# Linear attention with a sparse feed-forward layer: scores of two head groups in one go, and the fourth group of a step behind the output products that follow

## The chip, the cores and the metric

The kernel runs on one core of a Trainium2 chip. The metric is the device time of one execution in microseconds (us); "time" below means that. Five engines work side by side: PE (TensorE, the matmuls; PEld is its weight load), DVE (VectorE), ACT (ScalarE), POOL (GpSimd) and SP (SyncE, which here only issues DMAs). Each executes its own instructions in the order in which they were written; an instruction that must wait for another engine or for a DMA holds up everything behind it on its engine.

## The reference, cut to what matters

```python
x = x + _layernorm(_L0_attn_ref(_layernorm(x), Wq, Wk, Wv, Wo))      # x: 2 x 1024 x 512, float32
x = x + _layernorm(_L0_ffn_ref(_layernorm(x), w_gate, w_up, w_down))
...
# attention: 16 query heads, 4 key/value heads of 128; q and k get rotary positions, then elu + 1
state = state + k_s[..., :, None] * v_s[..., None, :]
z = z + k_s
num = jnp.einsum('bhe,bhed->bhd', q_s, state)
den = jnp.einsum('bhe,bhe->bh', q_s, z)[..., None] + EPS
out = num / den                                                       # then out @ Wo.T
# feed-forward: silu(x w_gate) * (x w_up), 2 of every 4 kept, then w_down
```

The attention is causal and linear: each position sees a running sum of k times v. A kernel may take it by chunks: within a chunk a masked matrix of scores q k, and from earlier chunks the state.

## The kernel before, in words

**Tiling.** The 1024 positions are cut into NC = 8 chunks of 128. The heads are taken in two passes of 8 query heads and 2 key/value heads, so there are STEPS = 16 steps: steps 0 to 7 are the first pass, 8 to 15 the second. A step n has four groups i = 0 to 3 (line 811: a batch b and a key/value head j), each with 4 query heads. After the attention follow four rounds of the feed-forward layer, which the change does not touch.

**Products.** Every large product (q, k and v, the output product "O" with Wo, the feed-forward products) is made by seven products of half-size factors (`chain`, line 507), in the order 1, 2, 6, 5, 7, 4, 3; their sums are made on ACT and DVE. `kv_products(n)` and `q_products(n)` make step n's k, v and q one step ahead, in step n-1. `o_products(n)` makes step n's output product; five of its seven products are issued in step n+1 and the last two (numbers 4 and 3) at the start of step n+2, by `run(previous, 2)` (line 1955).

**One group.** `features` (line 767) turns a raw q into its features on DVE, POOL and ACT. `moved` (line 629) then transposes it: DVE transposes 32x32 blocks into the tile `blocks`, SP writes them to a DRAM buffer `qb`, and four more DMAs of SP read it back as the tile `qT`. `scores(n, i)` (line 924) waits for `qT` of its group, makes the scores on PE into the PSUM tile `sc` (one buffer) and has DVE multiply them by the mask into `am` (one buffer). From the second chunk of a pass on, the scores of a group are two matmuls of a tile with 128 rows and 64 columns, 256 columns streamed in each. `attend(n, i)` (line 1022) multiplies q with the state (lines 1057) and the masked scores with v (line 1068, tiles of 64 rows), and makes the next group's change of the state (line 996); DVE and ACT then divide (`divided`, line 1089 and 1093), and `moved` sends the result through DRAM (`ob`) into the tile `of`, the left factor of the output products.

**The order on PE** is written out by hand in the loop over n (line 1920). In a step n of the first pass after the first it reads: last two output products of step n-2; products of q and k/v for step n+1 with `outputs(0)` and `outputs(1)` in between; two output products of step n-1; `outputs(2)`; two more; the transpose of k (`k_transposed(n+1)`); one more; `outputs(3)`. Steps 0 to 5 also hold two transposes of x (`step_input`). The function `outputs(i)` (line 1928) is:

```python
attend(n, i)
if i < 3:
    scores(n, i + 1)
elif 0 < n < STEPS - 1:
    scores(n + 1, 0)
```

So each `scores` stands alone behind an `attend`, one group ahead of its use. Behind the loop the last step is written out once more (lines 2030 to 2060), with `ffn_transposed` for the first transposes of the feed-forward layer.

**The order on the other engines** comes from a planner (`Plan`, line 36): processes ask for an engine with an estimated length and a rank, PE's issue times drive its clock, and the result is a fixed order per engine. Nothing in it is decided at run time. SP's one queue holds all DMAs: the reads and writes above, the weights of the second pass (`load_pass`, line 1269), x, the rotary table, and the preparation of the feed-forward weights, `prepare_all` (line 400), which loads 1 MB at a time, lets POOL make sums and stores 1 MB.

Of the kernel before, what the change touches and what calls it, by code (L numbers as in the profile page):

```python
# [13 lines left out]
ALU = mybir.AluOpType  # L14
PSUM = bass.MemoryType.PSUM

P = 128
B, S, DM = 2, 1024, 512
H, KVH, HD = 16, 4, 128
REP = H // KVH  # L20
DFF = 2048
NIC = DM // P
NC = S // P
# [88 lines left out]
def kernel(  # L112
# [16 lines left out]
    nc = tc.nc  # L129
# [9 lines left out]
    causal = const.tile([P, P], F32, name="causal")  # L139
# [11 lines left out]
    mask = const.tile([P, 64], F32, name="mask")  # L151
# [131 lines left out]
    STEPS = 2 * NC  # L283
# [175 lines left out]
    plan = Plan()  # L459
# [36 lines left out]
    def transposed(src, kind, *names):  # L496

        t, name, before = bank(kind, [P, 4, P])

        def issue():  # L500
            for j in range(4):
                nc.tensor.transpose(t[:, j, :], src[:, j, :], ident)

        plan.pe(0.45, issue, *before, *names)
        return t, name
# [304 lines left out]
    kf, kT, v1, qT = {}, {}, {}, {}  # L810
    GROUPS = ((0, 0), (1, 1), (0, 1), (1, 0))
# [109 lines left out]
    states, mids = {}, {}  # L921
    am, o = {}, {}

    def scores(n, i):
        b, j = GROUPS[i]
        plan.need(("qT", n, i), ("kT", n), *(("am", *k) for k in list(scored)))
        first = n % NC == 0
        sc = ps_sc.tile([P, 4, REP, 32], F32, tag="sc", name="sc")
        us = 4 if first else 2

        def issue():
            if first:
                nc.tensor.matmul(
                    sc.rearrange("p u h t -> p (u h t)"),
                    kT[n][:, 2 * b + j, :],
                    qT[n, i].rearrange("p u e -> p (u e)"),
                    start=True,
                    stop=True,
                )
                return  # L940
            for r in range(2):
                half_ = slice(64 * r, 64 * r + 64)
                nc.tensor.matmul(
                    sc[half_, 0:2].rearrange("p u h t -> p (u h t)"),
                    kT[n][:, 2 * b + j, half_],
                    qT[n, i][:, 2 * r : 2 * r + 2, :].rearrange("p u e -> p (u e)"),
                    start=True,
                    stop=True,
                    tile_position=(0, 64 * r),
                )  # L950

        def masked():
            yield "dve", 0.8 if first else 0.45, 0
            t = qp.tile([P, 4, REP, 32], F32, tag="am", name="am", bufs=1)
            of_ = (causal if first else mask).rearrange("p (u t) -> p u t", t=32).unsqueeze(2)
            nc.vector.tensor_tensor(
                t[:, 0:us], sc[:, 0:us], of_.broadcast_to([P, us, REP, 32]), ALU.mult
            )
            am[n, i] = t
            plan.signal(("am", n, i))  # L960

        plan.pe(0.87 if first else 0.6, issue, ("qT", n, i), ("kT", n), *(("am", *k) for k in scored))
        scored[:] = [(n, i)]
        plan.spawn(masked())

    scored, attended = [], []
# [156 lines left out]
    def o_factor(n, i):  # L1123

        k = (0, 2, 1, 3)[i]
        return factor(n, k, 2 if k in (0, 2) else 1)

    def o_free(n, i):

        k = n - 2 if i < 2 else n - 1  # L1130
        names = [("o", k, (1, 3, 2, 5)[i])] if k >= 0 else []
        return names + ([("of", k, 6)] if i == 2 and k >= 0 else [])

    def o_transposed(n, i, kind="a"):

        plan.need(("divided", n, i), *o_free(n, i))
        pt, name = transposed(o.pop((n, i)), kind, ("divided", n, i))

        def copy():
            yield "act", 0.65, 0  # L1140
            to = o_factor(n, i).rearrange("p h (u t) -> p h u t", t=32)
            nc.scalar.copy(to, pt.rearrange("p u (h t) -> p h u t", t=32))
            plan.signal(name)
            plan.signal(("of", n, i))

        plan.spawn(copy())
# [149 lines left out]
    def run(g, times):  # L1296
        for _ in range(times):
            next(g, None)
# [554 lines left out]
    with tc.manual_schedule(engines={E.PE, E.Pool, E.SP, E.DVE, E.Activation}):  # L1853
# [63 lines left out]
        run(qpr, 2)  # L1917
        opr = None
        part = 0
        for n in range(STEPS):  # L1920
            more = n + 1 < STEPS

            def next_part():
                nonlocal part
                plan.signal(("part", part))
                part += 1

            def outputs(i, n=n):
                if n not in (NC - 2, NC):
                    next_part()  # L1930
                attend(n, i)
                if i < 3:
                    scores(n, i + 1)
                elif 0 < n < STEPS - 1:
                    scores(n + 1, 0)

            if 0 < n < NC - 2:
                next_part()
            if n + 3 < NC:
                plan.spawn(load(n + 3, "x"))  # L1940
            if n + 2 < STEPS:
                if n + 2 < NC:
                    plan.spawn(step_normalize(n + 2, ("root", n)))
                else:
                    plan.spawn(step_input_again(n + 2))
            if n + 2 == NC:
                plan.spawn(load_pass(1, "wq", 2, 512, q_quarter, wq_dram, ("q", n + 1)))
                plan.spawn(load_pass(0, "wkv", 2, 256, kv_quarter, wkv_dram, ("k", n + 1)))
            elif n == NC:
                plan.spawn(load_pass(2, "wo", 4, 256, o_quarter, wo_dram, ("o", n - 1)))  # L1950
            previous, opr = opr, (o_products(n - 1) if n > 0 else None)
            if n > 0:
                plan.spawn(o_sums(n - 1))
            if n > 1:
                run(previous, 2)
            if not more:
                break
            kvp, qpr = kv_products(n + 1), q_products(n + 1)
            run(qpr, 1)
            if n == 0:  # L1960
                run(qpr, 1)
                run(kvp, 1)
                k_transposed(0, "e")
                q_transposed(0, 0, "e")
                run(qpr, 1)
            else:
                run(kvp, 1)
                run(qpr, 1)
                if n == 1:
                    k_transposed(1, "e")  # L1970
                    first_state(1, 0)
                elif n == NC + 1:
                    first_state(n, 0)
                run(qpr, 1)
                if n == 1:
                    scores(1, 0)
                    q_transposed(1, 1)
                    o_transposed(0, 3, "e")
            run(kvp, 1)
            plan.signal(("root", n))  # L1980
            if n > 0:
                outputs(0)
            else:
                scores(0, 0)
            if n + 2 < STEPS:
                plan.spawn(load(n + 2, "rope"))
            run(kvp, 1)
            run(qpr, 1)
            if n == 0:
                q_transposed(0, 1)  # L1990
                outputs(0)
            run(kvp, 1)
            run(qpr, 1)
            run(kvp, 1)
            if n == 0:
                q_transposed(0, 2)
                outputs(1)
                run(kvp, 1)
                run(qpr, 1)
                q_transposed(0, 3)  # L2000
                run(kvp, 1)
                step_input(2, 0, "a")
                outputs(2)
                step_input(2, 1, "a")
                run(qpr, 1)
                outputs(3)
            else:
                outputs(1)
                run(qpr, 1)
                run(kvp, 1)  # L2010
                run(qpr, 1)
                run(kvp, 1)
                run(opr, 2)
                outputs(2)
                if n + 2 < NC:
                    step_input(n + 2, 0, "a")
                run(opr, 2)
            if n + 2 == STEPS:
                plan.need(("prepared",), *(("features", n + 1, i) for i in range(4)))
                rctx.close()  # L2020
                begin_ffn()
            if n > 0:
                k_transposed(n + 1)
                run(opr, 1)
                if n + 2 < NC:
                    step_input(n + 2, 1, "a")
                outputs(3)


        o_transposed(n - 1, 3)  # L2030
        outputs(0)
        run(opr, 2)
        outputs(1)
        o_transposed(n, 0)
        for tt, kind in enumerate("eba"):
            ffn_transposed(tt, kind)
        run(opr, 3)
        o_transposed(n, 1)
        outputs(2)
        run(opr, 1)  # L2040
# [5 lines left out]
        opr = o_products(n)  # L2046
# [97 lines left out]
```

## Time and profile before

| what | value |
|---|---|
| median of three runs | 1283.44 us (1282.59 to 1283.59) |
| the profiled execution: time / span of its instructions | 1281.84 us / 1280.1 us |
| PE busy | 1251.9 us, 98% of the span |
| DVE, ACT, POOL busy | 67%, 36%, 27% |
| mean granted clock of PE | 0.996 |
| DMA queue of SP: packets' share of the 16 DMA engines | 62.4% |

The time around the span is 1.74 us. The profiled execution was 1.60 us faster than the median of the three runs. In the page's lines, "out<-in" names the tiles that an instruction writes and reads, Lnnn is a line of the kernel, and a figure in square brackets is idle time of the engine before the instruction with what ended it. Matmuls of 32-bit floats appear as two records each, so "x4" in the scores are two matmuls.

### The profile page before, as it was taken

The numbers are of one execution on the slowest core, as the hardware profiler recorded it, in microseconds if no ns is written. First come the engines' busy times: TensorE is split into PE (matmuls) and PEld (weight loads), VectorE is DVE, ScalarE is ACT, GpSimd is POOL, SyncE is SP. The second block draws the span as 40 slices with busy tenths as digits, with TensorE's granted clock in tenths as the row PEclk, the third lists the DMA queues.
The fourth block names the chain that finished last, engine by engine and source line by source line (L and its number), as shares of the span: only waits on it lengthen the run. The fifth ranks groups of instructions, "written<-read, shape, count | busy, mean of one in ns | idle before, by whom it ended". The sixth has DMA issues, their size and how long they took to land. (4 is left out here: it accounts for less than half of the span.)

```text
span 1280.1 us, 17815 instructions
## 1 busy us (share of the span) xinstructions
PE 1251.9 (98%) x6092; PEld 991.7 (77%) x6092; DVE 855.1 (67%) x1577; ACT 457.2 (36%) x909; POOL 341.5 (27%) x263
## 2 busy tenths in 40 slices
PE   7899999999999999999999999999999999999998
PEld 4566776777677766777678888888888888888886
DVE  7886877876566886778754588326971687426763
ACT  3653444443334444435443333113220343023211
POOL 4543443532232454455421101001100110010010
PEclk9998999999999999999999999999999999999999
DMA  7265678569767877676584499367546756465312
GB/s 266 94 232 191 224 233 274 194 214 280 243 219 206 290 235 232 233 241 207 174 244 149 138 253 257 115 190 220 152 136 209 245 152 193 154 190 173 109 41 91
DMA packets 280297, 252.60 MB, mean 197 GB/s; under 512 B 19216, under 2 KB 239376, under 8 KB 277520
## 3 DMA queue, kind: packets, MB, share of 16 engines
q1 hardware_dynamic: 278832, 249.51, 62.4%
q10 hardware_dynamic: 1376, 1.97, 0.5%
q8 instruction: 49, 0.80, 0.3%
q14 instruction: 40, 0.33, 0.1%
HBM read 179.83 MB, written 71.57 MB: 196 GB/s over the span
## 5 line engine op out<-in xcount | busy, mean ns | idle before, releaser
L532 ACT COPY u<-cb 128x512 f32<-128x512 f32 (+1 forms) x252 | 126.5, 503 | 464.6 <-PE cb L254 171.2
L1188 PE MATMUL cb<-wo,of 128*128 128x256 f32 x512 | 125.4, 388 | 1.3 <-PE ce L756 0.6
L796 POOL TENSOR_TENSOR qraw<-qraw,r 128x512 f32<-128x512 f32 x48 | 64.9, 1351 | 227.6 <-DVE qraw L787 202.7
L756 PE MATMUL cb<-wq,xf 128*128 128x512 f32 x256 | 121.9, 598 | 0.0
L254 PE MATMUL cb<-fxt,wgu 128*128 128x256 f32 x512 | 116.5, 379 | 1.0 <-issue 1.0
L254 PE MATMUL cb<-fxnT,wgu 128*128 128x256 f32 x512 | 116.8, 379 | 0.0
L1093 ACT ACTIVATE o<-nm,den 128x128 f32<-128x128 f32 x256 | 74.8, 369 | 116.1 <-DVE den L1089 116.0
L1188 PEld LDWEIGHTS cb<-wo,of 128*128 128x128 f32 x512 | 94.6, 192 | 23.6 <-issue 8.4
L254 PEld LDWEIGHTS cb<-fxt,wgu 128*128 128x128 f32 x512 | 97.2, 190 | 14.6 <-issue 1.4
L254 PEld LDWEIGHTS cb<-fxnT,wgu 128*128 128x128 f32 x512 | 97.2, 190 | 13.3
L1638 POOL TENSOR_TENSOR h<-h 128x512 f32<-128x512 f32 x16 | 25.6, 1602 | 305.4 <-DVE ht L1635 204.4
L453 POOL TENSOR_TENSOR wraw<-wraw 128x512 f32<-128x512 f32 x68 | 95.3, 1401 | 2.5
L543 DVE TENSOR_TENSOR y<-u,ce 128x256 f32<-128x256 f32 (+1 forms) x42 | 18.8, 450 | 109.6 <-ACT u L532 56.1
L756 PEld LDWEIGHTS cb<-wq,xf 128*128 128x128 f32 x256 | 47.2, 190 | 44.6 <-issue 42.8
L756 PEld LDWEIGHTS cb<-wkv,xf 128*128 128x128 f32 x256 | 48.1, 193 | 32.3 <-issue 25.1
L756 PE MATMUL cb<-wkv,xf 128*128 128x256 f32 x256 | 68.3, 390 | 0.1
L1188 PE MATMUL ce<-wo,of 128*128 128x256 f32 x256 | 61.3, 383 | 0.1
L804 DVE SCALAR_TENSOR_TENSOR qraw<-qraw,r 128x512 f32<-128x512 f32 x48 | 46.8, 977 | 20.6 <-ACT r L801 20.6
L756 PE MATMUL ce<-wq,xf 128*128 128x512 f32 x128 | 60.2, 593 | 0.0
L254 PE MATMUL ca<-fxnT,wgu 128*128 128x256 f32 x256 | 58.8, 379 | 0.0
L254 PE MATMUL ce<-fxnT,wgu 128*128 128x256 f32 x256 | 58.7, 379 | 0.0
L254 PE MATMUL ce<-fxt,wgu 128*128 128x256 f32 x256 | 58.7, 379 | 0.0
(189 smaller groups left out, 2433.0 us busy)
## 6 DMA issues: line engine op xcount, KB each, us to landing
wgu<-gs SPq DMA_DIRECT2D x64, 256.0 KB, 3.2
wgu<-us SPq DMA_DIRECT2D x64, 256.0 KB, 3.2
wd<-d_dram SPq DMA_DIRECT2D x32, 512.0 KB, 4.8
qb<-blocks SPq DMA_DIRECT2D x59, 256.0 KB, 2.4
qT<-qb SPq DMA_DIRECT2D x236, 64.0 KB, 2.5
ob<-blocks SPq DMA_DIRECT2D x58, 256.0 KB, 2.5
of<-ob SPq DMA_DIRECT2D x232, 64.0 KB, 2.2
xf<-xf SPq DMA_DIRECT2D x16, 896.0 KB, 4.8
```

The lines of the kernel that those rows point to most:

```text
L254: nc.tensor.matmul(bank[:, j, :].rearrange("p (w t) -> p w t", t=32), w[:, k, j, :], xf[xi][:, k], start=(start and j == 0 and k == 0), st ...
L453: nc.gpsimd.tensor_tensor(to, i0, i1, op)
L532: nc.scalar.copy(kept[i], b)
L543: nc.vector.tensor_tensor(dst[:, rows], kept[i][:, rows], b, ALU.add)
L756: nc.tensor.matmul(bank.rearrange("p h d -> p (h d)"), xf[n][:, xi, k, :], w[wi][:, k, :], start=(start and k == 0), stop=(k == 1), skip_g ...
L796: nc.gpsimd.tensor_tensor(u, u, r, ALU.add)
L804: nc.vector.scalar_tensor_tensor(f, u, 0.0, r, ALU.max, ALU.add)
L1093: nc.scalar.activation(t[:, u, :], nmv[:, u // 2, u % 2, 0:HD], AF.Copy, scale=den[:, u // 2, u % 2 : u % 2 + 1],)
L1188: nc.tensor.matmul(bank.rearrange("p h d -> p (h d)"), of[n, xi][:, k, :], weights[gp][2][wi][:, k, :], start=(start and k == 0), stop=(k ...
L1638: nc.gpsimd.tensor_tensor(b12, b22, b12, ALU.subtract)
```

## The change

`scores` takes one or two groups. For two groups it issues four matmuls in a row into the two halves of the same `sc` tile, waiting ahead of them for the `qT` of both; DVE masks the halves in two instructions. `paired(n)` says where: steps 3 to 14, but not step 8, which is the first of its pass. In a paired step groups 0 and 1 are scored together at the end of the step before, and groups 2 and 3 together behind `attend(n, 1)`.

`outputs(3)` of steps 2 to 14 moves: it now stands in the next step behind `run(previous, 2)`, that is, behind the two output products (numbers 4 and 3) that followed it. Step 2's first scores, `scores(2, 0)`, move from the end of step 1 to behind the first product of q in step 2. At the end, in step 15, one output product (not two) stands ahead of `o_transposed(14, 3)`, and two output products move ahead of the three `ffn_transposed`.

```diff
+    def scores(n, *groups):
+        names = [("qT", n, i) for i in groups] + [("kT", n)]
...
+            for g, i in enumerate(groups):
+                b, j = GROUPS[i]
+                for r in range(2):
+                    half_ = slice(64 * r, 64 * r + 64)
+                    nc.tensor.matmul(
+                        sc[half_, 2 * g : 2 * g + 2].rearrange("p u h t -> p (u h t)"),
+                        kT[n][:, 2 * b + j, half_],
+                        qT[n, i][:, 2 * r : 2 * r + 2, :].rearrange("p u e -> p (u e)"),
...
+        def paired(n):
+            return 3 <= n < STEPS - 1 and n % NC > 0
+
...
                 attend(n, i)
                 if i < 3:
-                    scores(n, i + 1)
-                elif 0 < n < STEPS - 1:
-                    scores(n + 1, 0)
+                    if not paired(n):
+                        scores(n, i + 1)
+                    elif i == 1:
+                        scores(n, 2, 3)
+                elif 1 < n < STEPS - 1:
+                    scores(n + 1, *(range(2) if paired(n + 1) else (0,)))
...
             if n > 1:
                 run(previous, 2)
+            if n > 2:
+                outputs(3, n - 1)
...
             run(qpr, 1)
+            if n == 2:
+                scores(2, 0)
...
-                outputs(3)
-
+                if n < 2:
+                    outputs(3)
 
+        run(opr, 1)
         o_transposed(n - 1, 3)
         outputs(0)
-        run(opr, 2)
+        run(opr, 1)
         outputs(1)
         o_transposed(n, 0)
+        run(opr, 2)
         for tt, kind in enumerate("eba"):
             ffn_transposed(tt, kind)
-        run(opr, 3)
+        run(opr, 1)
         o_transposed(n, 1)
```

More of the change, by code (lines that the diff above doesn't have):

```diff
@@ L922 @@
     am, o = {}, {}
-    def scores(n, i):
-        b, j = GROUPS[i]
-        plan.need(("qT", n, i), ("kT", n), *(("am", *k) for k in list(scored)))
+    def scores(n, *groups):
+        names = [("qT", n, i) for i in groups] + [("kT", n)]
+        names += [("am", *k) for k in scored]
+        plan.need(*names)
         first = n % NC == 0
         sc = ps_sc.tile([P, 4, REP, 32], F32, tag="sc", name="sc")
-        us = 4 if first else 2
+        us = 4 if first else 2 * len(groups)
         def issue():
             if first:
+                b, j = GROUPS[groups[0]]
                 nc.tensor.matmul(
@@ L935, in issue @@
                     kT[n][:, 2 * b + j, :],
-                    qT[n, i].rearrange("p u e -> p (u e)"),
+                    qT[n, groups[0]].rearrange("p u e -> p (u e)"),
                     start=True,
@@ L940, in issue @@
                 return
[L941 to L950, printed above, removed]
+            for g, i in enumerate(groups):
[6 more added lines that the diff above has]
+                        qT[n, i][:, 2 * r : 2 * r + 2, :].rearrange("p u e -> p (u e)"),
+                        start=True,
+                        stop=True,
+                        tile_position=(0, 64 * r),
+                    )
@@ L952, in masked @@
         def masked():
-            yield "dve", 0.8 if first else 0.45, 0
+            yield "dve", 0.8 if us == 4 else 0.45, 0
             t = qp.tile([P, 4, REP, 32], F32, tag="am", name="am", bufs=1)
[L955 to L960, printed above, removed]
@@ L962, in scores @@
-        plan.pe(0.87 if first else 0.6, issue, ("qT", n, i), ("kT", n), *(("am", *k) for k in scored))
-        scored[:] = [(n, i)]
+            if first:
+                of_ = causal.rearrange("p (u t) -> p u t", t=32).unsqueeze(2)
+                nc.vector.tensor_tensor(t, sc, of_.broadcast_to([P, 4, REP, 32]), ALU.mult)
+            else:
+                of_ = mask.rearrange("p (u t) -> p u t", t=32).unsqueeze(2)
+                for g in range(len(groups)):
+                    nc.vector.tensor_tensor(
+                        t[:, 2 * g : 2 * g + 2],
+                        sc[:, 2 * g : 2 * g + 2],
+                        of_.broadcast_to([P, 2, REP, 32]),
+                        ALU.mult,
+                    )
@@ L964, in scores @@
+            for g, i in enumerate(groups):
+                am[n, i] = t if first else t[:, 2 * g : 2 * g + 2]
+                plan.signal(("am", n, i))
+        plan.pe(0.87 if first else 0.15 + 0.45 * len(groups), issue, *names)
+        scored[:] = [(n, i) for i in groups]
         plan.spawn(masked())
```

## The prediction

> **What bounds the kernel now.** I read the page's first part (PE busy 1251.9 of 1280.1 us), then the list of what PE waited for, then PE's timeline around each place that the change touches, and last SP's timeline there. PE is the bound, and its idle time is short. The rows of the waits that lie in stages the change touches:
>
> ```profile
> PE 1251.9 (98%) x6092; PEld 991.7 (77%) x6092; DVE 855.1 (67%) x1577; ACT 457.2 (36%) x909; POOL 341.5 (27%) x263
> ...
> PE sc L943 <- DMA qT<-qb: 3.6, 2, 2.8
> ...
> PE ce L502 <- DVE fxn L189: 1.8, 1, 1.8
> ```
>
> So something on PE counts in full, and a wait that PE does not have now costs in full as well. PE's timeline at the end of step 1, its one long stop in the steady part:
>
> ```profile
> 106.42 0.39 PE L996 MATMUL nm<-v,kf 64*128 64x129 f32 x4
> 109.59 1.12 PE L943 MATMUL sc<-qT,kT 128*64 128x256 f32 x4 [2.77 <-DMA qT<-qb]
> 110.64 3.78 PE L1188 MATMUL cb<-wo,of 128*128 128x256 f32 x8
> 114.22 2.58 PE L1188 MATMUL ce<-wo,of 128*128 128x256 f32 x8
> 116.64 0.59 PE L756 MATMUL cb<-wq,xf 128*128 128x512 f32 x1
> ```
>
> The scores of step 2 wait 2.77 us for their qT, and the matmuls behind take longer than the same ones elsewhere. The table by stretches (length, busy time of the five engines, granted clock, DMA share, GB/s) says why: the clock.
>
> ```profile
> 106.00:110.00 4.00, 1.23 (x14) 0.95 (x16) 3.17 (x11) 1.14 (x4) 0.60 (x1) 0.85 0.58 172
> 110.00:116.00 6.00, 6.00 (x18) 4.27 (x15) 3.79 (x8) 1.63 (x3) 0.71 (x2) 0.53 0.65 208
> ```
>
> The trace's clock record puts half speed from 108.8 to 115.6, that is, it began 2.0 us after PE fell idle and lasted 6.8 us. The steady form, at the end of step 5:
>
> ```profile
> 277.80 0.61 PE L1057 MATMUL nm<-state,qT 128*128 128x129 f32 x4
> 278.24 0.61 PE L1057 MATMUL nm<-mid,qT 128*128 128x129 f32 x4
> 278.78 0.72 PE L1068 MATMUL nm<-v,am 64*128 64x129 f32 x8
> 279.33 0.39 PE L996 MATMUL nm<-v,kf 64*128 64x129 f32 x4
> 279.65 0.65 PE L943 MATMUL sc<-qT,kT 128*64 128x256 f32 x4
> 280.24 1.99 PE L1188 MATMUL cb<-wo,of 128*128 128x256 f32 x8
> 282.07 1.89 PE L1188 MATMUL ce<-wo,of 128*128 128x256 f32 x8
> ```
>
> From start to start an attend takes 1.85 us, the scores 0.59, the two output products 1.83 (0.10 of it behind the change of tile shape) and 1.72.
>
> **Part 1, pairs: a small gain.** One group's scores cost 0.59 us. A pass of 256 columns takes 1.72/8 = 0.215 us, and the two 64-column tiles run side by side (two matmuls, four records, in 0.59), so a second group directly behind the first adds two passes, 0.43. A pair saves 2 x 0.59 - (0.59 + 0.43) = 0.16 us. There are 11 paired steps with two pairs each: 22 x 0.16 = 3.4 us. Bounds: 0 (the second group costs its full 0.59) to 22 x 0.26 = 5.7 (the 0.10 us that the product behind the scores takes longer goes too). I take 3.4. DVE masks the same halves with the same number of instructions; its 0.40 us moves, and PE has at least 5 us between scores and their use.
>
> **Part 2, step 2's first scores later: the stop goes.** They now stand behind two output products and one product of q, 3.5 + 1.7 us later, so at about 112.0; their qT landed at 109.45. What is next there is ready (DVE's sums for the output products ended at 98.3 in its timeline). Gain: 2.77 idle, and at half clock 0.47 (1.05 for 0.58), 1.86 (3.58 for 1.72) and 0.70 (2.42 for 1.72): together 5.8 us. If the cover fails, at most this 5.8 stays.
>
> **Part 3, the end.** The 0.80 us wait of the scores (15, 1) at 654.8 and the 1.76 us wait for fxn at 663.8 go, since two output products, about 3.5 us, now stand ahead of each. New: `o_transposed(14, 3)` follows its attend by only 0.59 + 1.83 = 2.4 us, and from an attend's end to the last of its four divisions ACT and DVE took 3.4 us (279.65 to 283.03). That is about 1.0 us late. Net gain 1.5 us; bounds -1 to 2.6.
>
> **Part 4, the price: qT of group 1 is wanted 9.5 us earlier.** In the loop, the scores of (n, 1) stood behind `attend(n, 0)`, 12.9 us after those of (n, 0) (279.65 and 292.52 for step 6). Now they directly follow (n, 0), which itself moves back by two output products less one score: 3.46 - 0.59 = 2.9 us, and its own first passes 0.5. So (n, 1) is wanted at the old start of (n, 0) plus 3.4 us. Against that stands when the last of the four reads of qT(n, 1) landed in the trace of before. Lateness by step, if the landings stay: step 3: 154.08 + 3.4 against 159.49, 2.0 late; step 4: 4.6; 5: 1.2; 6 (283.0 against 289.59): 6.6; 7: 7.6; 9 (where (8, 3) keeps its place): 0.6; 10: 3.4; 13: 3.2; steps 11, 12 and 14: in time by 0.4 to 1.0. Sum 29 us. Group 3 is wanted only 0.25 us earlier than group 2 was and lands in time, or within 0.3 us.
>
> Why so late? SP's queue for step 6 (start, length, issue):
>
> ```profile
> 271.10 0.40 SPq L429 DMA_DIRECT2D wraw<-in_w_gate_dram  x1
> 271.59 0.46 SPq L640 DMA_DIRECT2D qb<-blocks  x1
> 274.46 0.32 SPq L640 DMA_DIRECT2D ob<-blocks  x1
> 277.46 1.74 SPq L647 DMA_DIRECT2D qT<-qb  x4
> 279.25 0.43 SPq L640 DMA_DIRECT2D qb<-blocks  x1
> 279.78 0.38 SPq L640 DMA_DIRECT2D ob<-blocks  x1
> 280.20 3.77 SPq L647 DMA_DIRECT2D of<-ob  x4
> 284.08 0.37 SPq L727 DMA_DIRECT2D xf<-xf  x1
> 284.56 2.80 SPq L647 DMA_DIRECT2D qT<-qb  x4
> ```
>
> DVE had the blocks of group 1 ready at 276.2; SP wrote them at 279.25, because group 2's reads ahead waited for a write that shares the DMA engines with a 1 MB load, and read them at 284.56, behind the `of` reads and a store of 0.9 MB. Undisturbed, a write and four reads took 5.6 us (2.1 and 3.4); here 13.3.
>
> In the built order of the changed kernel DVE comes to group 1's transpose at the same place (one mask of 0.4 us less ahead of it). SP's order differs by step, and I correct the lateness: step 6 the same order (6.2); step 4 with the x load (0.5 MB, 1.3 us) ahead as well (5.9); steps 10 and 13 without the 1 MB load between write and read (1.4 and 1.2); step 7 with its write ahead of group 2's reads, and with weight loads that start earlier against PE, because PE stopped in step 6 (3.1); steps 3 and 5 (1.0 and 0.3); steps 9, 11 and 14 with group 3's write or reads of `of` put ahead (2.0, 1.5 and 0.6). Sum 23 us. Each is one wait of PE with everything behind it. Bounds: from 0 (every landing quickened to 5.6 us behind DVE, which would be in time in every step) to 35.
>
> A stop of over 2 us also lowers the clock, by the row above: half speed lasts until 8.8 us after PE fell idle, so a stop of s costs (8.8 - s)/2 more. For steps 4, 6 and 7: 1.4 + 1.3 + 2.9 = 5.6. Bounds 0 and 15 (five such stops).
>
> [...]
>
> **Sum.** 23 + 5.6 - 3.4 - 5.8 - 1.5 = +17.9 on the profiled 1281.84: 1299.7. The median of before lies 1.6 higher, so I predict 1301.
>
> **Rivals.**
> *Faster: the landings follow the demand.* If SP and the DMA engines serve group 1 within the undisturbed 5.6 us (DVE's transpose ended 9.7 to 12.9 us after step n's last q product, and the scores would want qT 17 to 19 us after it), no wait stands: 1283.44 - 10.7 = 1273. It decides where waits and clock together stay under 10.7 us. For it: in six of eleven steps my lateness is under 1.5 us. Against it: in steps 4 and 6 the order keeps 1 MB transfers ahead. Chance 0.28.
> *Much slower.* The stops in the first pass shift into each other, and most fall over 2 us: 29 + 6 of waits and 15 of clock less 10.7, +39: 1323. Against it: a stop gives DMA time to catch up. Chance 0.08.
> *Even.* Waits and clock come to 8 to 13 us: 1283. Chance 0.05.
> *The pair saves nothing* (a second wait between its matmuls keeps the 0.59): 3.4 us off the gains, 1304; it lies inside my forecast.
>
> **Numbers.** Forecast (slower, its own range 1286 to 1314) 0.59, with the others 1. Faster by over 0.2% (about what a measurement of this kernel can tell from no change): 0.28; within: 0.05; slower: 0.67. The range reaches into the faster rival: 1272 to 1314; beyond lie the much slower case and the edge of the faster one.
>
> **What the profile will show.** Right: in the list of PE's waits, "sc <- DMA qT" goes from 2 rows to about 8, some 20 us in all, the longest in steps 4 and 6, with the clock under 1 behind them; no stop at 107; fxn's wait gone. A pair of scores takes 1.0 us from start to start. Wrong: if SP's row for group 1's reads stands within 6 us of DVE's transpose in steps 4, 6 and 7, Part 4 falls, and with it the sign.

## The result, and the profile after

The changed kernel took **1319.48 us** (median of four runs, 1318.96 to 1319.72) beside 1283.01 us for the kernel before (1281.48 to 1283.59): ratio 1.0291, 95% interval 1.0279 to 1.0303. That is 36.5 us slower, where the prediction said 18, and above its range. The profiled execution took 1319.43 us with a span of 1317.7; against the 1281.84 of before it lost 37.6 us.

The page's first part and the list of PE's waits (total, times, longest):

```profile
PE 1263.2 (96%) x6092; PEld 995.9 (76%) x6092; DVE 867.3 (66%) x1577; ACT 456.9 (35%) x909; POOL 340.0 (26%) x263
```

```profile
PE sc L947 <- DMA qT<-qb: 26.0, 7, 6.4
...
PE cb L1201 <- ACT u L532: 5.3, 9, 1.3
```

Before, the last of these rows was:

```profile
PE cb L1188 <- ACT u L532: 0.2, 1, 0.2
```

The same 6092 matmul records now keep PE busy 11.3 us longer (1263.2 for 1251.9), and PE is idle 26.3 us longer (54.5 for 28.2). So the loss has two halves to explain. The idle half stands in the list: the waits for `qT` went from 3.6 to 26.0 us, waits for ACT's copy `u` from 0.2 to 5.3, and the wait for `fxn` is gone. The busy half is the clock. The table by stretches (length, then busy time of PE, PEld, DVE, ACT, POOL; granted clock; DMA share; GB/s), taken at the six places where the trace's clock record shows half speed while PE works:

```profile
157.11:163.94 6.83, 5.49 (x11) 2.52 (x12) 1.10 (x3) 0.58 (x1) 0.00 (x0) 0.50 0.84 317
208.31:215.14 6.83, 5.02 (x9) 2.17 (x10) 0.76 (x2) 0.15 (x1) 0.00 (x0) 0.50 0.77 285
300.47:303.88 3.41, 3.41 (x6) 1.48 (x5) 0.76 (x2) 0.00 (x0) 0.00 (x0) 0.50 0.80 288
344.84:351.67 6.83, 6.29 (x12) 3.18 (x13) 0.86 (x3) 0.59 (x1) 0.00 (x0) 0.50 0.65 215
433.59:437.00 3.41, 3.41 (x7) 1.38 (x8) 0.76 (x2) 0.00 (x0) 0.00 (x0) 0.50 0.68 235
522.34:525.75 3.41, 3.41 (x5) 1.35 (x5) 0.99 (x5) 0.01 (x1) 0.00 (x0) 0.50 0.54 171
```

PE worked 27.0 us at half speed, half of it lost: 13.5 us. Before, it was one such stretch with 6.0 us of work, 3.0 lost:

```profile
108.78:115.61 6.83, 6.02 (x16) 4.26 (x17) 4.32 (x9) 2.76 (x7) 1.31 (x2) 0.50 0.61 188
```

The difference, 10.5, is nearly all of the 11.3.

What a stop looks like, at the pair of step 4 (PE's timeline). The first group's matmuls run at 203.04; the second group's wait 6.43 us, *inside* the pair, and the q product behind takes 3.58 us from start to start instead of 1.82:

```profile
203.04 0.65 PE L947 MATMUL sc<-qT,kT 128*64 128x256 f32 x4
210.12 1.12 PE L947 MATMUL sc<-qT,kT 128*64 128x256 f32 x4 [6.43 <-DMA qT<-qb]
211.17 3.78 PE L756 MATMUL cb<-wq,xf 128*128 128x512 f32 x4
214.75 1.23 PE L756 MATMUL cb<-wkv,xf 128*128 128x256 f32 x4
```

Two things went as meant. Step 2's stop is gone: its scores at 112.37 start without a wait.

```profile
110.56 1.88 PE L756 MATMUL cb<-wq,xf 128*128 128x512 f32 x4
112.37 0.65 PE L947 MATMUL sc<-qT,kT 128*64 128x256 f32 x4
112.95 1.13 PE L756 MATMUL cb<-wkv,xf 128*128 128x256 f32 x4
```

And a pair whose data is there takes 1.01 us from start to start (494.89 to 495.90, groups 2 and 3 of step 10; all eleven pairs of groups 2 and 3 took as long):

```profile
494.89 1.08 PE L947 MATMUL sc<-qT,kT 128*64 128x256 f32 x8
495.90 1.12 PE L756 MATMUL cb<-wq,xf 128*128 128x512 f32 x2
```

The wait for ACT is new, and the prediction has no line for it. PE's timeline of before and of after between the steps 9 and 10 of the loop:

```profile
440.19 1.89 PE L1188 MATMUL cb<-wo,of 128*128 128x256 f32 x8
441.92 0.61 PE L1057 MATMUL nm<-state,qT 128*128 128x129 f32 x4
...
444.36 1.99 PE L1188 MATMUL cb<-wo,of 128*128 128x256 f32 x8
```

```profile
468.77 1.89 PE L1201 MATMUL cb<-wo,of 128*128 128x256 f32 x8
471.36 1.99 PE L1201 MATMUL cb<-wo,of 128*128 128x256 f32 x8 [0.69 <-ACT u L532]
...
474.91 0.61 PE L1070 MATMUL nm<-state,qT 128*128 128x129 f32 x4
...
476.77 1.37 PE L947 MATMUL sc<-qT,kT 128*64 128x256 f32 x8
```

ACT's timeline of after between the two:

```profile
470.41 0.63 ACT L801 ACTIVATE r<-r 128x512 f32<-128x512 f32 x1
470.95 0.35 ACT L532 COPY u<-cb 128x256 f32<-128x256 f32 x1
```

In `chain`, product 4 is accumulated onto the sum of products 1, 6 and 7 in the same PSUM bank, after ACT has copied that sum out (`snapshot`). Product 7 of step n-1 ends step n, product 4 begins step n+1, and `outputs(3)` stood between them. The change took it away, so ACT's copy lies bare: PE waits for it in nine places, 0.46 us at the least and up to 1.25.

### The profile page after: what moved, and what is told of

It reads as the page before. It is cut to its first block, busy times and chain, and to the rows that moved or that the text cites. A ratio compares the mean times of both kernels' runs of the same rounds, so it can differ in the third digit from the quotient of the medians.

```text
span 1317.7 us, 17775 instructions
## 1 busy us (share of the span) xinstructions
PE 1263.2 (96%) x6092; PEld 995.9 (76%) x6092; DVE 867.3 (66%) x1577; ACT 456.9 (35%) x909; POOL 340.0 (26%) x263
## 5 line engine op out<-in xcount | busy, mean ns | idle before, releaser
L756 PE MATMUL cb<-wq,xf 128*128 128x512 f32 x256 | 132.9, 644 | 0.0
L254 PEld LDWEIGHTS cb<-fxnT,wgu 128*128 128x128 f32 x512 | 97.2, 190 | 13.3
L804 DVE SCALAR_TENSOR_TENSOR qraw<-qraw,r 128x512 f32<-128x512 f32 x48 | 50.1, 1046 | 17.1 <-ACT r L801 16.9
L947 PE MATMUL sc<-qT,kT 128*64 128x256 f32 x224 | 35.5, 416 | 26.1 <-DMA qT<-qb 26.0
```

The costliest lines, as they stand in the source:

```text
L254: nc.tensor.matmul(bank[:, j, :].rearrange("p (w t) -> p w t", t=32), w[:, k, j, :], xf[xi][:, k], start=(start and j == 0 and k == 0), st ...
L756: nc.tensor.matmul(bank.rearrange("p h d -> p (h d)"), xf[n][:, xi, k, :], w[wi][:, k, :], start=(start and k == 0), stop=(k == 1), skip_g ...
L804: nc.vector.scalar_tensor_tensor(f, u, 0.0, r, ALU.max, ALU.add)
L947: nc.tensor.matmul(sc[half_, 2 * g : 2 * g + 2].rearrange("p u h t -> p (u h t)"), kT[n][:, 2 * b + j, half_], qT[n, i][:, 2 * r : 2 * r + ...
```

## The experiments

Ratios are against the kernel before, in the same session; the changed kernel has 1.0291.

**1. No pairs; 2. the pair of groups 2 and 3 only; 3. the pair of 0 and 1 only; 4. pairs, but `outputs(3)` at its old place.**

```diff
 def paired(n):                                   # 1
-    return 3 <= n < STEPS - 1 and n % NC > 0
+    return False
...
-                    if not paired(n):            # 2, with scores(n + 1, 0) alone below
+                    if not paired(n) or i == 0:
...
-                    if not paired(n):            # 3, with no scores(n, 2, 3)
+                    if not paired(n) or i > 0:
...
-            if n > 2:                            # 4
-                outputs(3, n - 1)
...
-                if n < 2:
-                    outputs(3)
+                outputs(3)
```

> The changed kernel with no pairs: every group's scores stand alone again, (n, 1) behind attend(n, 0); the moved outputs(3), step 2's late scores and the tail stay. Theory (qT of group 1 wanted too early): the seven waits of PE for qT (26.0 us) and the half clock behind them (27 us of work at half speed, 13.5 us) go, the pairs' saving (3.4 us, of which the waits inside the pairs took back some 2) goes too: about 1319.5 - 26 - 13.5 + 1.5 = 1281 us, 1278 to 1285, with the clock at 1. Rival (the later outputs(3) is the price: it also delays DVE's mask and DMAs of group 3): 1305 us or more, with waits of over 15 us left.

> The changed kernel with the pair of groups 2 and 3 only; groups 0 and 1 stand alone. Theory (only the pair of groups 0 and 1 comes before its data): no wait for qT(n, 3) over 0.3 us, and 11 x 0.16 = 1.7 us under the kernel with no pairs: about 1279 us. Rival (both pairs come too early): 1290 us or more, with waits behind attend(n, 1).

> The changed kernel with the pair of groups 0 and 1 only; groups 2 and 3 stand alone. Theory: all of the waits (26 us) and of the half clock stay, and 1.7 us of the pairs' saving goes: about 1321 us, 1317 to 1326. Rival (both pairs come too early): 1300 us or less.

> The changed kernel with outputs(3) back at the end of its own step; pairs, step 2 and tail as changed. The pair of groups 0 and 1 is then wanted two output products, 3.5 us, earlier still, while PE's waits for ACT at the first output product (5.3 us) go. Theory: each of the 11 pairs waits up to 3.5 us more, 26 + 34 = 60 us of waits if the landings stay, and more of them halve the clock: about 1350 us, 1335 to 1362. Rival (the later outputs(3) is the price): under 1319 us.

Measured: 1289.81 us, 1.0052 (1.0034 to 1.0071); 1289.75, 1.0053 (1.0038 to 1.0068); 1320.91, 1.0294 (1.0278 to 1.0309); 1347.97, 1.0502 (1.0472 to 1.0532). So the whole loss beyond half a per cent is the pair of groups 0 and 1; the pair of 2 and 3 changes nothing that can be measured (1.7 us expected); and at the old place, where the pair is wanted 3.5 us earlier, the waits grow from 26.0 to 53.1 us (some 60 expected), with a stop at each of the eleven pairs and one of 0.7 us in step 15:

```profile
PE sc L947 <- DMA qT<-qb: 53.1, 12, 8.9
```

But the kernel with no pairs was expected at 1281 and came out 9 us above. Its waits show no `qT`, and the bared copy in ten places:

```profile
PE cb L1201 <- ACT u L532: 6.0, 10, 1.2
...
PE cb L1201 <- DVE of L1178: 2.1, 1, 2.1
```

**5. Step 2 and tail alone** (no pairs, `outputs(3)` at its old place: edits 1 and 4 together). **6. A late pair**, `outputs(3)` at its old place. **7. A late pair**, `outputs(3)` as changed. The late pair:

```diff
                 run(kvp, 1)
                 run(qpr, 1)
+                if paired(n):
+                    scores(n, 0, 1)
```

**8. No loads:** ten 1 MB loads of feed-forward weights are left out.

> The kernel before with step 2's late scores and the reordered tail alone: no pairs, outputs(3) at its old place. Theory: the stop at 107 us and its half clock go (5.8 us) and the tail gives about 1.5: 1283.5 - 7.3 = 1276 us. The kernel with no pairs but with the moved outputs(3) took 1289.8; the second theory formed on it is that the move costs the rest, 13 us, by PE's waits for ACT's copies at the first output product (6.0 us in ten waits, up to 1.2) and for factors of the output product, which outputs(3) covered at its old place. Rival (step 2's or the tail's change costs): 1285 us or more here.

> outputs(3) at its old place; the pair (n, 0, 1) behind three more products of step n (q, k/v, q: 4.3 us later than in the changed kernel); pair (n, 2, 3), step 2 and tail as changed. Theory (only the lateness of qT(n, 1) matters): the stops of the changed kernel less 4.3 us each: step 4 some 2.1, step 9 0.2, step 3 0.0, the others none; so the kernel of step 2 and tail alone (1276) - 3.4 + 2.3 + at most 1.7 of clock: 1275 to 1277 us, faster than the kernel before. Rival (scores directly behind products of q or DVE's two masks too late for attend(n, 0), which follows 2.6 us behind): 1285 us or more, with waits at attend(n, 0).

> The changed kernel with the pair (n, 0, 1) behind three more products, 4.3 us later, and outputs(3) at its new place. Theory: the stops for qT go to about 2.3 us; the waits for ACT at the first output product (5 to 6 us) and what else the move costs stay: the kernel with no pairs (1289.8) - 3.4 + 2.3 = 1289 us. Rival (the move costs nothing by itself): 1277 us.

> The changed kernel without the 1 MB loads of the feed-forward weights from the eighth unit on (ten loads left out, so the feed-forward layer gets wrong weights; the sums and the 1 MB stores stay). Theory (1 MB loads ahead of group 1's reads make them late): the waits in steps 6, 9 to 13 shrink where such a load lay just ahead (step 11: 2.6 us), those of steps 3 and 4 (loads that stay) do not; 26 us of waits fall to some 20, 1319 to 1310. Rival (features on POOL and DVE, or the order of SP's queue, set the landing): waits stay at 24 us or more.

Measured: 1280.33 us, 0.9984 (0.9968 to 1.0000); 1280.49, 1.0003 (0.9981 to 1.0025); 1293.9, 1.0091 (1.0069 to 1.0114); one run of 1315.8. Without pairs the move of `outputs(3)` makes 0.9984 into 1.0052, with a late pair 1.0003 into 1.0091: 0.7 to 0.9%, 9 to 11 us. With the pair at the changed kernel's place it does the opposite (1.0502 becomes 1.0291), because it gives `qT` 3.5 us more. The late pair takes the waits for `qT` from 53.1 to 3.5 us (old place) and from 26.0 to 2.7 (new place), about as expected; but kernel 6 was to be faster than the kernel before, at 1275 to 1277, and is not, and kernel 7 came out 5 us above its 1289. These ten loads matter little: without them step 11's stop is gone, but PE still waits 22.9 us for `qT` in six stops, nearer to the rival's 24 than to 20.

And kernel 5 gained 2 us (0 to 4) where 7.3 were expected. Its profile has two new stops, for DVE's sum for the output product, of 4.1 and 2.1 us, at 190 and 279 us.

**9. Group 1 first on DVE; 10. with `outputs(3)` at its old place too; 11. group 1 first with late pairs at the old place; 12. the transpose of k behind product 7.** The trace shows two reasons why `qT(n, 1)` lands late. Step 6 of the changed kernel, on ACT, DVE, SP and PE:

```profile
274.95 0.63 ACT L801 ACTIVATE r<-r 128x512 f32<-128x512 f32 x1
```

```profile
270.05 0.65 DVE L543 TENSOR_TENSOR qraw<-u,ce 128x512 f32<-128x512 f32 x1
...
287.30 1.13 DVE L804 SCALAR_TENSOR_TENSOR qraw<-qraw,r 128x512 f32<-128x512 f32 x1
288.46 0.71 DVE L634 STREAM_TRANSPOSE blocks<-qraw 128x512 f32<-128x512 f32 x1
```

```profile
291.43 0.43 SPq L640 DMA_DIRECT2D qb<-blocks  x1
...
294.90 2.83 SPq L647 DMA_DIRECT2D qT<-qb  x4
```

```profile
299.86 0.65 PE L947 MATMUL sc<-qT,kT 128*64 128x256 f32 x4 [3.67 <-DMA qT<-qb]
```

ACT's exponential is there at 275.6; DVE takes it up at 287.3. Between group 1's sum at 270.05 and its transpose the planner has put 27 instructions of other work. Behind the transpose SP's queue takes another 10.6 us until the reads have landed, 5.0 more than the 5.6 of an undisturbed write and four reads.

```diff
-                f = yield from features(src, n, done, None, int(n + i > 0))
+                f = yield from features(src, n, done, None, int(n + i > 0 and i != 1))
...
-        yield "dve", 0.8
+        yield "dve", 0.8, int(name[0] != "qT" or name[2] != 1)
...
-                k_transposed(n + 1)              # 12
                 run(opr, 1)
+                k_transposed(n + 1)
```

> The changed kernel with group 1 ahead of the other groups in the planner (rank 0 for its features and its transpose): between the sum that makes group 1's raw q and its transpose stand 11 to 14 instructions on DVE, not 25 to 31. In the changed kernel's trace of step 6 ACT had group 1's exponential ready at 275.6 and DVE took it up at 287.3, and DVE was the last engine that could have come earlier. Theory (DVE's order makes qT(n, 1) late): the transpose comes 6 to 10 us earlier, all seven stops for qT and the half clock behind them go, and the kernel comes to that with the pair of groups 2 and 3 alone (1289.8) less 1.7: 1288 us, 1284 to 1292. Rival (SP's queue and the 1 MB transfers make it late): 15 us or more of waits stay, 1305 us or more.

> As the last kernel, and outputs(3) back at its old place, so that the pair is wanted 3.5 us earlier still; without the rank this kernel took 1348.0 us, with twelve waits of 53.1 us (longest 8.9). Theory (DVE's order makes qT late): a landing 6 to 10 us earlier leaves at most 3 us of waits, and the waits for ACT at the first output product are not there: the kernel without pairs at the old place (1280.3) - 3.4 + 3 = 1280 us, 1274 to 1286. Rival (SP's queue): over 1310 us.

> The kernel with the late pair and outputs(3) at its old place (1280.5 us, 1274 to 1290), with group 1 ahead in the planner. Theory: its 3.5 us of waits for qT go and nothing else moves: 1278 us, 1273 to 1283. Rival (DVE's sums for the output products, which now come behind, are late): over 1284 us, with PE waiting for the factors of the output product.

> The changed kernel with the transpose of k (0.44 us on PE) moved behind the output product number 7, so that it stands between that product and number 4, which waits for ACT's copy of number 7's sum (5.3 us in nine waits, 0.46 us the least). Theory (the move of outputs(3) bared ACT's copy): most of the nine waits shrink by 0.44, so about 4 us go, 1315.5 us. Rival (the waits are for an ACT that is late for other reasons): the waits stay at 5 us, 1319 us.

Measured: 1329.15 us, 1.0380 (1.0350 to 1.0409); 1295.42, 1.0116 (1.0082 to 1.0149); 1290.81, 1.0067 (1.0050 to 1.0085); 1320.42, 1.0295 (1.0273 to 1.0318). Kernel 9 is the telling one. On DVE, step 6's group 1 is now done 7.1 us after its sum (19.1 before the edit):

```profile
265.20 0.65 DVE L543 TENSOR_TENSOR qraw<-u,ce 128x512 f32<-128x512 f32 x1
...
270.91 0.68 DVE L804 SCALAR_TENSOR_TENSOR qraw<-qraw,r 128x512 f32<-128x512 f32 x1
271.62 0.71 DVE L634 STREAM_TRANSPOSE blocks<-qraw 128x512 f32<-128x512 f32 x1
```

and the list of waits has no row for `qT` any more. So DVE's order alone can bring the landing in time. That SP's queue is not a cause does not follow. In the changed kernel's seven stops the landing came 8.7 to 13.3 us behind the transpose's end, and what this has over 5.6 (3.1 to 7.7 us) is more than the stop each time: a quick path through SP would have been enough as well. And in kernel 9 that path changed too: over the eleven paired steps it took 89 us, 109 before the edit. But the time got worse, which no theory had: DVE's sums for the output product are now the late ones.

```profile
PE cb L1201 <- DVE of L1178: 25.0, 8, 4.3
PE cb L1201 <- ACT u L532: 9.2, 12, 3.0
```

Two more stops are new, of 5.9 us for a read of `of` and of 4.6 us for ACT. At the old place, where the output products come later against those sums, the same edit brings 1.0502 down to 1.0116, with 9.8 us of waits for them left, 4.9 for `qT` and 4.6 for ACT; 1280 was expected, so that was short by 15; kernel 11, with the same 9.8 us, came out above its rival's bound. Kernel 12 shrank the waits for ACT's copy from 5.3 to 2.1 us, about as expected, but not the time: the transposes now wait for ACT's copy of k (1.5 us before the edit), and an output product for DVE's sum.

```profile
PE ca L502 <- ACT kT L858: 3.4, 5, 0.7
PE cb L1201 <- DVE of L1178: 3.2, 1, 3.2
...
PE cb L1201 <- ACT u L532: 2.1, 7, 0.5
```

**13. Step 2 alone; 14. the tail alone** (each put into the kernel before); **15. and 16. kernels 10 and 11 with DVE's three sums for the output product first as well** (the same edit at all three):

```diff
 def o_sums(n):
...
-        yield "dve", 0.8
+        yield "dve", 0.8, 0
```

> The kernel before with step 2's late scores alone. DVE's order has the sum for the output product (L1165 here) 16 places behind the one ahead of it in two steps where the kernel before has 1 and 3, as the kernel with step 2 and tail has. Theory (the planner's new order on DVE gives the gain back): stops at about 190 and 279 us, 6 us, with up to 3 us of half clock; 1283 - 5.8 + 6 to 9: 1281 to 1286 us. Rival (the gain of 5.8 is there and the tail gave it back): 1277 us.

> The kernel before with the reordered tail alone. Theory: waits of 2.6 us go (0.8 for the scores (15, 1), 1.8 for the transposes of the feed-forward layer), a new one of about 1 us comes for the factor of the output product: 1.5 us faster, 1281. Rival (the tail costs): over 1284 us.

> Pairs at the old place of outputs(3), with group 1 and DVE's three sums for the output product ahead in the planner. Without the sums it took 1295.4 us and waited 9.8 us for those sums in four stops. Theory (DVE's order decides which is late, and DVE, busy 66%, has room for both): the 9.8 us and some half clock go, 1284 us, 1280 to 1287. Rival (on DVE one's gain is another's delay): waits for other results of DVE come, 1292 us or more.

> Late pairs, outputs(3) at its old place, with group 1 and the sums ahead in the planner; without the sums it took 1290.8 us. Theory: the 9.8 us of waits for the sums go: 1280 us, 1276 to 1283. Rival: other waits come, 1287 us or more.

Measured: 1284.2 us, 1.0014 (1.0000 to 1.0027); 1279.49, 0.9975 (0.9960 to 0.9990); 1295.33, 1.0108 (1.0077 to 1.0140); **1277.08, 0.9958 (0.9939 to 0.9977)**. Step 2's move by itself gains nothing: it shifts the planner's times, and DVE's order sets the sum for the output product 16 places behind its predecessor in two steps, where the kernel before has 3 in both. The stops stand where the orders differ:

```profile
PE cb L1188 <- DVE of L1165: 6.2, 2, 4.1
```

The tail's change is worth 3.2 us (1.3 to 5.1; 1.5 expected). With pairs at the old place and both first on DVE, the waits for the sums are gone but 19.2 us of waits for `qT` are back, in four stops; the time is the rival's, though these waits are not for DVE. With late pairs both are in time, and the kernel is 0.2 to 0.6% faster than the one before.

**17. The fastest kernel without pairs, beside itself.**

```diff
-                    scores(n, 0, 1)
+                    scores(n, 0)
...
-                    if not paired(n):
-                        scores(n, i + 1)
-                    elif i == 1:
-                        scores(n, 2, 3)
+                    scores(n, i + 1)
```

> The fastest kernel with no pairs: scores(n, 0) at the late place, the other groups each behind an attend as in the kernel before; step 2, tail and DVE's order (group 1 and the sums first) as there. Theory (a pair saves 0.16 us, 22 pairs 3.4 us, once their data is there): 3.4 us over the kernel with pairs beside it. Rival (pairs are worth nothing): within 1 us of it.

> The fastest kernel so far, beside the one without pairs: 1277 us, 1274 to 1280, and under the kernel before by 0.3 to 0.5 per cent (0.9958 in its first session, interval 0.9939 to 0.9977).

Measured: 1282.69 us, 1.0007 (0.9994 to 1.0020) without pairs; **1274.22, 0.9946 (0.9928 to 0.9964)** with. The scores themselves take 39.8 us in all on PE without pairs (start to start, idle left out) and 36.5 with: 3.3 us, the 3.4 of the prediction. So 3.4 was expected, 8 measured. The rest shows in the trace without pairs (the slowest of its twelve executions): PE waits 3.1 and 2.1 us for ACT in two places, and 8.9 us of output products run at half clock. That this is again a matter of order is argued, not shown. The same kernel with its first scores at their old place (kernel 15 without pairs) gives no time, since its fixed order deadlocks.

## Why the prediction was wrong

**The direction and the mechanism were right:** the kernel is slower because the pair of groups 0 and 1 asks for `qT(n, 1)` before it lands (experiments 1 to 4 and 9). The size was half. By its steps:

**Part 1 (3.4 us) was right** as a price: a pair takes 1.01 us (predicted 1.02), and 3.3 us were measured on PE between experiment 17's two kernels. In the changed kernel it bought nothing: a pair with a stop inside it is no pair.

**Part 2 (5.8 us) was right at its place.** The first attend of step 2 starts at 118.22, before at 123.51, though the trace of after ran 0.26 us late at 98 us: 5.6 us. But the prediction did not ask what the stop had been *giving*. In step 3 the pair stands at 153.47 and its `qT` lands at 158.3; before, it landed at 159.5. From the trace of before the pair would have stood at 157.6 (154.08 and two output products, 3.55). So PE came 4.2 us earlier, the landing 1.2. I had set step 3's lateness at 1.0 from a trace in which PE was still later; it was 4.3. Alone, the move even costs 0 to 3.5 us (experiment 13), by DVE's new order.

**Part 3 (1.5 us)** measured 3.2, with an interval (1.3 to 5.1) that holds 1.5.

**Part 4's waits were right in sum, 26.0 for 23,** and only roughly right by step (predicted, then measured): step 3 1.0, 4.3; step 4 5.9, 6.4; step 6 6.2, 3.7; step 7 3.1, 2.4; step 9 2.0, 4.5; step 11 1.5, 2.6; step 14 0.6, 2.0; the other four, 0 to 1.4, came under 0.3. The near sum is partly luck. The working moves the pair back by two products "less one score", but no score comes off: product 4 starts at 471.36 and the pair at 476.77, which is two products (3.55) and an attend (1.86). With 3.55 in place of 2.9 its own landings give some 17 us, not 23. The reason it gave, SP's queue, is one of two: by the traces a quick path there, or an earlier place in DVE's order (9), would each have ended the waits, and their shares stay open. Of the 1 MB loads, the ten left out in experiment 8 were worth 3 us.

**Part 4's clock is the step that failed first:** "For steps 4, 6 and 7: 1.4 + 1.3 + 2.9 = 5.6". Seven stops, not three, were over 2 us, and six of them halved the clock: 13.5 us, 8 more than the 5.6. The rule for the price was wrong as well (see the last section): by (8.8 - s)/2 the seven would have cost 17.8.

**A term was missing, put at nothing:** the moved `outputs(3)` was priced by what it delays and never by what it *covered*. It covered ACT's copy between products 7 and 4; that is 5.3 us of waits in the changed kernel. In the pairs of kernels that differ in the move alone the whole move costs 9 to 11 us, of which 6.0 and 7.0 are waits for this copy.

So, on the prediction's own sum: 17.9 + 3 (waits) + 8 (clock) + 5 (copy) = 34 of the measured 37.6. Most of the rest is the pairs' 3.4: over the whole kernel PE spent as long on scores as before (40.2 and 40.3 us start to start, idle left out): a pair with a stop inside took 1.24 us, and 1.7 where the clock was halved too.

**The rivals:** faster (0.28) was far off, since in seven of eleven steps the landing did not follow the demand. "Much slower" (1323, 0.08) came nearest, 3.5 us away, but partly by luck: it had 35 us of waits that were 26, and 15 of clock that were 13.5; the copy and the pairs' lost gain, which it did not have, filled the gap. Its chance was too small.

**Why the waits for DVE's sum wander** between kernels that differ little, the traces show. In all twenty there are 320 such sums. In 24 steps the sum stands 15 to 29 places behind the sum ahead of it on DVE, and PE waited for it in just these 24; in the other 296 it stands at most 13 places behind, and PE never waited. So these waits are DVE's order, in kernels 9 and 10 as in 13.

What stays open: kernel 15's 19.2 us of waits for `qT`. DVE had group 1 first there, and yet the four reads landed 6.9 to 17.7 us behind the transpose; what held them on SP's queue was not tried. Open too is why the runs of one kernel spread (1274 to 1290 us in experiment 6).

## What to carry to other kernels

When a block of work is moved, list what stood behind its cover (here one copy of 0.35 us between two products) as well as what it delays; both are in the timeline before the change. When a stop is taken away, count it as time lost to every landing behind it. And where a planner sets the order of a busy engine, an early demand is a question to that order first: giving one result the first place made another late, and of the kernels with pairs only the one that moved the demand as well (experiment 16) gained anything.

## What the runs showed of the hardware

A stop's price on the clock did not follow its length. The changed kernel's seven stops for `qT`, in steps 3, 4, 6, 7, 9, 11 and 14, lasted 4.33, 6.43, 3.67, 2.44, 4.52, 2.57 and 2.04 us. With the first six the trace's clock record has half speed for 6.83, 6.83, 3.41, 6.83, 3.41 and 3.41 us, with the seventh none; with the stop of 2.77 us in the kernel before it has 6.83. The starts of those six half-speed stretches lie 51.20, 92.16, 44.37, 88.75 and 88.75 us apart, 15, 27, 13, 26 and 26 times 3.413 us. In the 3.41 us just ahead of the seven half-speed stretches PE was busy 0.00 to 1.51 us. Counted on in steps of 3.413 us from them, the stretch with step 14's stop has PE busy 1.96 us, and in the kernel before the one with the wait for `fxn` 1.65. Step 7, with the 1.51, and step 14:

```profile
341.43:344.84 3.41, 1.51 (x15) 0.93 (x14) 1.14 (x4) 1.14 (x4) 0.10 (x1) 1.00 0.69 219
344.84:348.26 3.42, 2.88 (x6) 1.16 (x7) 0.86 (x3) 0.00 (x0) 0.00 (x0) 0.50 0.78 265
648.63:652.04 3.41, 1.96 (x7) 0.88 (x8) 2.36 (x7) 1.01 (x4) 0.14 (x2) 1.00 0.49 141
```

The kernel before:

```profile
661.75:665.16 3.41, 1.65 (x14) 1.28 (x13) 3.37 (x8) 1.77 (x5) 0.79 (x1) 1.00 1.11 287
```

Behind the 1.51 us came half speed (0.50 in the row below it), behind the 1.65 and the 1.96 full (1.00 in the next 3.41 us of both). That the place of a stop goes into its price is my estimate from these stops; what sets the clock was not shown. The prediction drew the wrong lesson from its one stop of 2.77 us, a threshold and a price by the stop's length: by it PE would have worked 6.2 us at half speed behind the stop of 2.57 us and 6.8 behind that of 2.04, and the trace has 3.41 and none.
